# Another order for layer 3's side steps in a four-layer kernel: when they are issued beside the scan, which decay comes first, and the norm within one chunk

## The chip, the cores and the metric

The kernel runs on one core of a Trainium2 chip. The metric is the time of one launch on the device in microseconds (us): the median of several runs, and beside it the one execution that the hardware profiler recorded. Five engines work side by side, each in the order of its own instruction stream: PE (TensorE, matmuls), DVE (VectorE), ACT (ScalarE), POOL (GpSimd) and SP (SyncE), which here issues all DMAs.

## The reference, cut to what matters

Four layers run one after the other on an input of 4 images, 128 channels, 64 x 64 points: an attention with a threshold, a selective scan, a softmax attention, and a selective scan in both directions with a group norm. The change is about the last one and about the scan loop that layers 1 and 3 share.

```python
u = silu(conv(u) + conv_b)                       # 256 inner channels, from xf @ Win
x_dbl = u @ Wx                                   # dt (8), Bm (16), Cm (16)
delta = softplus(dt @ Wdt + bdt)
dA  = exp(delta * A)                             # for each channel and each of 16 states
dBu = delta * Bm * u
h = dA_l * h + dBu_l                             # step by step along 16384 points
y = sum over states of h * C_l
y = (y + u * D) * silu(z)
out = y @ Wout                                   # forward pass plus flipped backward pass
xn = (xg - mu) * rsqrt(var + 1e-5) * gn_w + gn_b # 4 groups of channels in each image
return silu(xn) + x
```

## The kernel before

Layer 3 (`layer3`, from line 1423) cuts the 16384 points into 16 chunks of T = 1024 and goes through them forward, then backward: 32 chunks, numbered 0 to 31 below. A chunk has J = 2 blocks (two halves of the 256 channels), and a block 16 tiles. A tile holds 128 rows, 8 channels times 16 states, by 1024 points. So a chunk has 32 tiles, numbered 0 to 31 below, and the layer 1024. Layer 1 has the same number of tiles, 256 for each image, in blocks that are summed four by four.

`scan_stream` (line 640) is the loop over tiles. All its engines are pinned to the program's order (`InOrder`, line 101), so what is written first is done first on each engine. For tile i it does, in this order:

- `carried(i - 2)`: ACT copies the last column of h to the carry, and with that lets go of the h buffer (four of them);
- `spread(i + 1)`: two matmuls put the rows of du of the next tile on all its partitions, in one of two PSUM buffers named db;
- `decayed_apart(i + 1)` and then `decayed(i + 2)`: ACT's exponentials. Every fourth tile (i % 4 == 3) is "apart": there the rows of delta are taken from PSUM and the decay is done in place (db<-db), the rows of du come by DMA, and POOL multiplies them by B (`driven`, x<-row, three tiles ahead). In all others the rows of delta come by DMA (da<-row), and DVE multiplies db by B;
- `load_for(i + 3)`: SP issues the next loads of rows, 512 KB each, into five buffers. That gives the row of tile i + 5 unless it is apart, and the row of tile i + 6 if it is apart;
- DVE's product (not if apart) and the scan; POOL's product of h and C (p<-h);
- the loads of B and C for the next block at n == 6 of a block (`reps`);
- at n == 4 `begun`: two matmuls start the sums of a block with u times D;
- the side steps of this tile; then, in every fourth tile, `summed`: 16 matmuls add four older tiles' p.

When a block is over, `done` multiplies silu(z) by its sums on DVE, at n == 3 of the next block.

The side steps of layer 3 are written out by tile in a plan (`into`, line 1708; `run`). Steps of one tile run in the order in which they were added: those of `prep` are added at the start, those of `post` and `finish` when a chunk ends. `prep(K)` (line 1469) gives the steps that make chunk K's inputs, during the chunk before it: `taps` and `silu(.., "u")` for u, `rows_a` and `rows_b` for B, C and dt, `step_a` and `step_b` for delta, then `time_steps` (line 788) for each block as todo(j, 0) to todo(j, 6), and `gate` with `silu(.., "z")`. The seven todo steps are:

- 0, `times`: SP stores 96 rows of delta, POOL computes du = delta * u, SP stores 32 rows of du;
- 1, `other`: ACT copies delta over those 32 rows of du. It can only run when the store has read them;
- 2, `high`: ACT casts to bf16;
- 3 and 5, `minus`: PE computes what the cast left over, in the two PSUM banks named misc; 4 and 6, `rest`: ACT casts that. After 6, SP issues 12 DMAs that place the three bf16 parts in `parts`, which `spread` reads.

`post(K)` (line 1566) makes the chunk's output (o_ps, yo) and stores it; `finish(b)` (line 1592) runs when a backward chunk completes an image: it loads the image's four tiles of r, sums them, takes the mean, loads them again for the squares, computes scale and shift, and loads them a third time for silu, the residual (POOL) and the store. yo, r and res share two SBUF buffers (`scratch`). Three images finish beside the scan of later chunks, and the last one after the scan. A plan entry above 31 falls in the chunk after.

Of the kernel before, what the change touches and what calls it, by code (L numbers as in the profile page):

```python
# [115 lines left out]
class Net:  # L116
# [523 lines left out]
    def scan_stream(self, pools, blocks, side, early=lambda k, n: None):  # L640

        pe, dve, act, pool, sp = self.pinned()  # L650
        rows, tmp, psd, pst = pools
        S, E = self.SPREAD, self.EIGHT
        O, Q, G = S // E, P // S, P // E

        order = [q * O + o for o in range(O) for q in range(Q)]
        items = [(k, n) for k in range(len(blocks)) for n in range(G)]
        W = self.T
        AHEAD = 3
        db, da, p, h, row = {}, {}, {}, {}, {}
        total = {}  # L660

        def apart(i):
            return i % Q == Q - 1

        def of(i):
            k, n = items[i]
            return blocks[k], order[n]

        def decay(t, src, i):
            B, g = of(i)  # L670
            act.activation(t, src, AF.Exp, scale=B.decay[:, g : g + 1])
            da[i] = t

        def spread(i):

            if i < len(items):
                B, g = of(i)
                db[i] = psd.tile([P, W], F32, name="db", tag="db")
                for j in range(W // NB):
                    s = bass.ts(j, NB)  # L680
                    pe.matmul(db[i][:, s], self.sel[:, g % O, :], B.parts[:, g // O, s], start=True, stop=True)

        def decayed(i):
            if i < len(items) and not apart(i):
                decay(tmp.tile([P, W], F32, name="da", tag="da"), row.pop(i), i)

        def decayed_apart(i):
            if i < len(items) and apart(i):
                t = db.pop(i)
                decay(t, t, i)  # L690

        def load(i):
            if i < len(items):
                B, g = of(i)
                row[i] = rows.tile([P, W], F32, name="row", tag="row", bufs=5)
                from_ = B.rows[g * E : (g + 1) * E, :]
                sp.dma_start(out=row[i], in_=from_.unsqueeze(0).to_broadcast([G, E, W]))

        def load_for(t):

            if not apart(t + 2):
                load(t + 2)
            if apart(t + AHEAD):
                load(t + AHEAD)

        x = {}

        def driven(i):
            if i < len(items) and apart(i):
                x[i] = tmp.tile([P, W], F32, name="x", tag="x", bufs=1)  # L710
                pool.tensor_tensor(x[i], row.pop(i), of(i)[0].b_rep, ALU.mult)

        def begun(B):
            if B.first:
                B.totals[0] = pst.tile([P, W], F32, name="total", tag="total")
                for j in range(W // NB):
                    s = bass.ts(j, NB)
                    pe.matmul(B.totals[0][:, s], B.diag_d, B.u[:, s], start=True, stop=False)

        def summed(i):  # L720

            k, n = items[i]
            B = blocks[k]
            for j in range(W // NB):
                s = bass.ts(j, NB)
                for m in range(i, i + Q):
                    g = of(m)[1]
                    r = (g // O) * S
                    pe.matmul(
                        B.totals[0][r : r + S, s], self.gather[:, g % O, :], p[m][:, s],  # L730
                        start=False, stop=(B.last and n == G - Q),
                    )
            for m in range(i, i + Q):
                del p[m]

        def carried(i):
            B, g = of(i)
            act.copy(B.carry[:, g : g + 1], h[i][:, B.at : B.at + 1])
            del h[i]

        blocks[0].reps()
        for i in range(-2, AHEAD):
            load_for(i)
        spread(0)
        decayed(0)
        decayed(1)
        for i, (k, n) in enumerate(items):
            B, g = of(i)
            if i > 1:
                carried(i - 2)  # L750
            spread(i + 1)
            decayed_apart(i + 1)
            decayed(i + 2)
            load_for(i + AHEAD)
            if not apart(i):
                x[i] = db.pop(i)
                dve.tensor_tensor(x[i], B.b_rep, x[i], ALU.mult)
            if n == 3 and k and blocks[k - 1].last:
                blocks[k - 1].done(blocks[k - 1].totals.pop(0))
            early(k, n)  # L760
            h[i] = tmp.tile([P, W], F32, name="h", tag="h", bufs=4)
            dve.tensor_tensor_scan(
                h[i][:, B.way], da[i][:, B.way], x[i][:, B.way], B.carry[:, g : g + 1], ALU.mult, ALU.add,
            )
            del da[i], x[i]
            p[i] = tmp.tile([P, W], F32, name="p", tag="p", bufs=7)
            pool.tensor_tensor(p[i], h[i], B.c_rep, ALU.mult)
            driven(i + AHEAD)
            if n == 6 and k + 1 < len(blocks):
                blocks[k + 1].reps()  # L770
            if n == 4:
                begun(B)
            side(k, n)
            if i % Q == 1 and i > Q:
                summed(i - 1 - Q)
        carried(len(items) - 2)
        carried(len(items) - 1)
        summed(len(items) - Q)
        blocks[-1].done(blocks[-1].totals.pop(0))

# [642 lines left out]
    def layer3(self):  # L1423
# [4 lines left out]
        with self.pool("l3w", 1) as big, self.pool("l3", 2) as work, self.pool("l3t", 2) as tmp, \  # L1428
# [40 lines left out]
            def prep(K):  # L1469
# [82 lines left out]
                def todo(j, i):  # L1552
# [3 lines left out]
                    8: [begin, taps(0, 0)], 10: [taps(0, 1)], 11: [silu(0, "u")],  # L1556
                    12: [taps(1, 0)], 14: [taps(1, 1)], 15: [silu(1, "u")],
                    16: [rows_a], 17: [rows_b], 18: [step_a(0)], 19: [step_b(0)],
                    20: [todo(0, 0)], 21: [todo(0, 1)], 22: [todo(0, 2), step_a(1)], 23: [step_b(1)],
                    24: [todo(1, 0), todo(0, 3)], 25: [todo(0, 4)],  # L1560
                    26: [todo(1, 1), gate(0)], 27: [silu(0, "z")],
                    28: [todo(1, 2), todo(0, 5)], 29: [todo(0, 6)],
                    30: [gate(1)], 31: [silu(1, "z")],
                }, {0: [todo(1, 3)], 1: [todo(1, 4)], 2: [todo(1, 5)], 3: [todo(1, 6)]}

            def post(K):
                lo = K.ch * T
                held = {}

                def a(c):  # L1570
                    def go():
                        held[c] = misc("o_ps")
                        for j in range(J):
                            pe.matmul(held[c], self.WoutT[:, j, :], K.sz[:, j, bass.ts(c, NB)], start=(j == 0), stop=(j == J - 1))
                    return go

                def b():
                    t = scratch("yo")
                    for c in range(C):
                        s = bass.ts(c, NB)  # L1580
                        if K.forward:
                            act.copy(t[:, s], held[c])
                        else:
                            dve.tensor_tensor(t[:, s], held[c], K.yf[:, s], ALU.add)
                    sp.dma_start(out=self.y3[:, lo : lo + T], in_=t)

                slots = {4: [a(0)], 6: [a(1)], 7: [b]}
                if not K.forward and lo % L == 0:
                    slots |= finish(lo // L)
                return slots  # L1590

            def finish(b):
# [66 lines left out]
                        sp.dma_start(out=self.out[b, :, bass.ts(m, T)], in_=r)  # L1659
                    return go  # L1660

                slots = {20: [over_group("sum"), mean], 52: [over_group("dev")], 53: [scale], 54: [shift]}
                for at, f in ((8, sums), (22, squares)):
                    for m in range(M + 1):
                        slots[at + m] = ([f(m - 1)] if m else []) + ([part(m)] if m < M else [])
                for m in range(M):
                    slots[55 + 3 * m] = [part(m)]
                    slots[56 + 3 * m] = [silus(m)]
                    slots[57 + 3 * m] = [outs(m)]
                return slots  # L1670

            chunks = []
            for forward in (True, False):
                for ch in range(NT) if forward else reversed(range(NT)):
                    K = Chunk()
                    K.ch, K.forward, K.number, K.turn = ch, forward, len(chunks), len(chunks) % 2
                    K.blocks = []
                    for j in range(J):
                        B = Block()
# [36 lines left out]
            for i, K in enumerate(chunks):  # L1716
                now, gates = prep(K)
                into(i - 1, now)
                into(i, gates)
                if i > 1:  # L1720
                    into(i - 2, {4: [lambda K=K: fetch(K)]})
                else:
                    fetch(K)
                if not K.forward:
                    into(i, {NS: [lambda K=K: behind(K)]})
# [102 lines left out]
```

## Time and profile before

| what | us |
|---|---|
| median of 3 runs | 11183.19 (11176.51 to 11188.2) |
| the profiled execution | 11183.87 |
| its span, first to last instruction | 11182.1 |
| layer 3: first scan starts | 7254.8 |
| layer 3: last scan ends | 11103.1 |
| chunk 3 (forward), first scan to next chunk's first scan | 7603.55 to 7719.85 |
| layer 1's scans, four images | 863.3, 903.1, 903.4, 892.5 |

| engine | busy us | share of the span |
|---|---|---|
| PE | 8629.2 | 77% |
| DVE | 9239.8 | 83% |
| ACT | 6252.6 | 56% |
| POOL | 8143.9 | 73% |

The time is the device's time for one launch; the span is what lies between the first and the last instruction that the profiler recorded, so 1.8 us lie around it. A group's line in the page gives the line of the source (L111 is the helper through which every pinned instruction passes, so groups are told apart by the names of their tiles), the engine, the operation, what it writes and reads with shapes, the count, then busy time and mean duration of one in ns, and last the idle time of the engine just before these instructions with what ended most of it. An arrow points to what was waited for: "<-ACT db" is a wait until ACT had written db. A timeline line gives the start, the duration, the engine, and in brackets the idle time before it. SP's lines show when a DMA was issued, not when it landed.

### The profile page before, as it was taken

To read this page: it belongs to the slowest core of one execution; us is meant where nothing else is said; L and a number is where in the kernel's file an instruction comes from. 1 tells how busy PE (TensorE), PEld (TensorE's weight loads), DVE (VectorE), ACT (ScalarE), POOL (GpSimd) and SP (SyncE) were. 2 spreads that over 40 slices of the span, in tenths; PEclk is the share of its full clock that TensorE was granted. 3 is DMA by queue.
4 is the path that set the end of the run, shared out by engine and by line. 5 is a ranking of instruction groups with operands and counts; after the bars stand their busy time and mean duration, and the time that the engine had idled before them with its cause. 6 is when DMAs were issued, how large, how long until landed. Compare 5 with 4: busy or idle time off the path is not lost. (4 is left out here: it accounts for less than half of the span.)

```text
span 11182.1 us, 91225 instructions
## 1 busy us (share of the span) xinstructions
PE 8629.2 (77%) x28104; PEld 3091.9 (28%) x28104; DVE 9239.8 (83%) x6438; ACT 6252.6 (56%) x9435; POOL 8143.9 (73%) x3566
## 2 busy tenths in 40 slices
PE   8986668987787997787997877877777777766665
PEld 3331113332222332222332222322222222222221
DVE  7859997869997876997886997198888988888876
ACT  3324445646664655664664665456566565656564
POOL 6748885748886766886774886088888888777776
PEclk9997779998998998998998988888888888878887
DMA  1017771008872006874005885177777777778776
GB/s 28 15 48 190 191 175 32 15 26 204 202 195 61 17 12 169 204 197 105 15 13 122 201 200 134 41 190 184 191 180 188 189 186 192 195 188 199 191 197 164
DMA packets 502953, 1522.34 MB, mean 136 GB/s; under 512 B 83432, under 2 KB 91144, under 8 KB 502464
## 3 DMA queue, kind: packets, MB, share of 16 engines
q1 hardware_dynamic: 502464, 1516.51, 54.9%
q8 instruction: 223, 3.65, 0.1%
q14 instruction: 266, 2.18, 0.1%
HBM read 1327.38 MB, written 125.94 MB: 130 GB/s over the span
## 5 line engine op out<-in xcount | busy, mean ns | idle before, releaser
L111 POOL TENSOR_TENSOR p<-h,c_rep 128x1024 f32<-128x1024 f32 x2048 | 4808.0, 2356 | 1312.4 <-DVE h L111 1209.8
L111 DVE TENSOR_TENSOR_SCAN h<-da,carry,db 128x1024 f32<-128x1024 f32 x1536 | 3603.4, 2346 | 232.7 <-ACT da L111 50.9
L111 PE MATMUL db<-parts,sel 96*128 96x512 bf16 x4096 | 1414.4, 432 | 1587.9 <-DVE h L111 1443.2
L111 DVE TENSOR_TENSOR db<-b_rep,db 128x1024 f32<-128x1024 f32 x1536 | 1856.5, 1209 | 399.3 <-PE db L111 217.8
L111 ACT ACTIVATE da<-row,A 128x1024 f32<-128x1024 f32 x1536 | 1752.8, 1144 | 127.0 <-DMA row<-d 126.8
L111 POOL TENSOR_TENSOR e<-e,bound 128x1024 f32<-128x1024 f32 x512 | 1242.1, 2428 | 567.2 <-DVE e L111 567.1
L111 ACT ACTIVATE db<-db,A 128x1024 f32<-128x1024 f32 x512 | 556.9, 1088 | 1779.6 <-PE db L111 1736.0
L111 DVE TENSOR_TENSOR_SCAN h<-db,carry,x 128x1024 f32<-128x1024 f32 x512 | 1194.7, 2333 | 201.6 <-ACT db L111 195.9
L111 POOL TENSOR_TENSOR x<-row,b_rep 128x1024 f32<-128x1024 f32 x512 | 1207.5, 2358 | 6.3 <-DMA row<-d 6.3
L111 PEld LDWEIGHTS <-sel 96*128 96x128 bf16 x4096 | 325.4, 102 | 3083.1 <-DVE h L111 1694.9
L111 PE MATMUL total<-p,gather 128*32 128x512 f32 x8192 | 1158.7, 679 | 21.0 <-POOL p L111 21.0
L111 PE MATMUL lg<-q,k 128*128 128x512 f32 x2048 | 1026.2, 625 | 153.6 <-DVE e L111 153.2
L111 ACT ACTIVATE e<-e 128x1024 f32<-128x1024 f32 x512 | 540.9, 1057 | 1046.9 <-POOL e L111 1046.9
L111 PE MATMUL acc<-e,values 128*128 128x512 f32 x1536 | 884.1, 668 | 180.7 <-ACT e L111 157.6
L111 PE MATMUL acc<-t,vT 128*128 128x512 f32 x2048 | 955.9, 593 | 6.4 <-DVE t L111 3.3
L111 DVE TENSOR_TENSOR t<-lg,ncut 128x1024 f32<-128x1024 f32 x512 | 624.8, 1220 | 292.3 <-PE acc L111 260.5
L111 ACT ACT_TABLE_LOAD x593 | 760.8, 1283 | 99.0 <-DMA r<-y 71.6
L111 POOL TENSOR_TENSOR t<-t,e 128x1024 f32<-128x1024 f32 x256 | 609.8, 2382 | 47.4 <-ACT t L111 47.4
L111 ACT ACTIVATE e<-gq,below,fcol 128x512 f32<-128x512 f32 x768 | 609.9, 805 | 60.6 <-PE acc L111 60.3
L111 PE MATMUL rest_ps<-du,ident 128*128 128x512 f32 x640 | 480.0, 842 | 206.0 <-ACT sz L111 120.4
L111 ACT ACTIVATE junk<-gp,ntop,fcol 128x512 f32<-128x512 f32 x768 | 619.5, 807 | 27.6 <-DMA gp<-g 14.9
L111 DVE SCALAR_TENSOR_TENSOR e<-t,lg 128x1024 f32<-128x1024 f32 x512 | 619.1, 1209 | 2.5
(214 smaller groups left out, 10085.3 us busy)
## 6 DMA issues: line engine op xcount, KB each, us to landing
row<-d SPq DMA_DIRECT2D x2048, 512.0 KB
parts<-split SPq DMA_DIRECT2D x960, 64.0 KB
b_rep<-bc SPq DMA_DIRECT2D x96, 512.0 KB
c_rep<-bc SPq DMA_DIRECT2D x96, 512.0 KB
d<-delta SPq DMA_DIRECT2D x80, 384.0 KB
r<-y SPq DMA_DIRECT2D x48, 512.0 KB
xq<-in_x SPq DMA_DIRECT2D x64, 256.0 KB
q<-q SPq DMA_DIRECT2D x64, 256.0 KB
```

Of the source, the lines that this page charges most:

```text
L111: return self.tc.keep_in_program_order(method(*args, **kwargs))
```

## The change

Four things change.

In `scan_stream` the two matmuls of `begun` move from tile n == 4 of a block, ahead of the side steps, to just before the block's first `summed`, which comes after the side steps of tile n == 5. And `decayed(i + 2)` is issued before `decayed_apart(i + 1)`, no longer after it. Both touch layers 1 and 3.

In `prep` the steps from tile 20 on are laid out anew. `other` of block 0 moves from tile 21 to tile 23, three tiles behind `times`; `times` of block 1 moves from 24 to 22; all `rest` steps of both blocks end at tiles 27 and 31, where before block 1's last four steps ran in tiles 0 to 3 of the chunk itself. The gates change places with them: they move from tiles 26 to 31 of the chunk before into tiles 0, 2, 6 and 7 of the own chunk.

In `post` and around it the output matmuls and yo move from tiles 4, 6, 7 to 3, 4, 5, and the load of xt for the chunk after next from tile 4 to 7.

In `finish` the norm of an image, which ran over tiles 8 to 66 counted from the chunk after the image's last, runs over tiles 6 to 37: sums in 6 to 10, mean in 17, squares in 18 to 22, the group's deviation in 24, scale and shift together in 25, the last pass in 26 to 37. No operation is added or dropped.

```diff
-        def begun(B):
-            if B.first:
+        def summed(i):
+
+            k, n = items[i]
+            B = blocks[k]
+            if n == 0 and B.first:
                 B.totals[0] = pst.tile([P, W], F32, name="total", tag="total")
                 for j in range(W // NB):
                     s = bass.ts(j, NB)
                     pe.matmul(B.totals[0][:, s], B.diag_d, B.u[:, s], start=True, stop=False)
...
             spread(i + 1)
+            decayed(i + 2)
             decayed_apart(i + 1)
-            decayed(i + 2)
             load_for(i + AHEAD)
...
-            if n == 4:
-                begun(B)
             side(k, n)
...
-                    20: [todo(0, 0)], 21: [todo(0, 1)], 22: [todo(0, 2), step_a(1)], 23: [step_b(1)],
-                    24: [todo(1, 0), todo(0, 3)], 25: [todo(0, 4)],
-                    26: [todo(1, 1), gate(0)], 27: [silu(0, "z")],
-                    28: [todo(1, 2), todo(0, 5)], 29: [todo(0, 6)],
-                    30: [gate(1)], 31: [silu(1, "z")],
-                }, {0: [todo(1, 3)], 1: [todo(1, 4)], 2: [todo(1, 5)], 3: [todo(1, 6)]}
+                    20: [todo(0, 0), step_a(1)], 21: [step_b(1)], 22: [todo(1, 0)], 23: [todo(0, 1), todo(0, 2)],
+                    24: [todo(0, 3)], 25: [todo(0, 4)], 26: [todo(0, 5), todo(1, 1)],
+                    27: [todo(0, 6), todo(1, 2)], 28: [todo(1, 3)], 29: [todo(1, 4)], 30: [todo(1, 5)],
+                    31: [todo(1, 6)],
+                }, {0: [gate(0)], 2: [silu(0, "z")], 6: [gate(1)], 7: [silu(1, "z")]}
...
-                slots = {4: [a(0)], 6: [a(1)], 7: [b]}
+                slots = {3: [a(0)], 4: [a(1)], 5: [b]}
...
-                slots = {20: [over_group("sum"), mean], 52: [over_group("dev")], 53: [scale], 54: [shift]}
-                for at, f in ((8, sums), (22, squares)):
+                slots = {17: [over_group("sum"), mean], 24: [over_group("dev")], 25: [scale, shift]}
+                for at, f in ((6, sums), (18, squares)):
                     for m in range(M + 1):
                         slots[at + m] = ([f(m - 1)] if m else []) + ([part(m)] if m < M else [])
                 for m in range(M):
-                    slots[55 + 3 * m] = [part(m)]
-                    slots[56 + 3 * m] = [silus(m)]
-                    slots[57 + 3 * m] = [outs(m)]
+                    slots[26 + 3 * m] = [part(m)]
+                    slots[27 + 3 * m] = [silus(m)]
+                    slots[28 + 3 * m] = [outs(m)]
...
-                    into(i - 2, {4: [lambda K=K: fetch(K)]})
+                    into(i - 2, {7: [lambda K=K: fetch(K)]})
```

More of the change, by code (lines that the diff above doesn't have):

```diff
@@ L718, in begun @@
                     pe.matmul(B.totals[0][:, s], B.diag_d, B.u[:, s], start=True, stop=False)
-        def summed(i):
-            k, n = items[i]
-            B = blocks[k]
             for j in range(W // NB):
```

## The prediction

> **What bounds the kernel now.** I read the page first, then the vector engine's waits over layer 3, then one chunk's timeline, then the DMA share in stretches of it. The page's groups:
>
> ```profile
> L111 POOL TENSOR_TENSOR p<-h,c_rep 128x1024 f32<-128x1024 f32 x2048 | 4808.0, 2356 | 1312.4 <-DVE h L111 1209.8
> L111 DVE TENSOR_TENSOR_SCAN h<-da,carry,db 128x1024 f32<-128x1024 f32 x1536 | 3603.4, 2346 | 232.7 <-ACT da L111 50.9
> L111 DVE TENSOR_TENSOR db<-b_rep,db 128x1024 f32<-128x1024 f32 x1536 | 1856.5, 1209 | 399.3 <-PE db L111 217.8
> L111 ACT ACTIVATE da<-row,A 128x1024 f32<-128x1024 f32 x1536 | 1752.8, 1144 | 127.0 <-DMA row<-d 126.8
> L111 ACT ACTIVATE db<-db,A 128x1024 f32<-128x1024 f32 x512 | 556.9, 1088 | 1779.6 <-PE db L111 1736.0
> ```
>
> The reader is to see that three tiles of four need a product and a scan on DVE (1.21 + 2.35, 3.60 from scan start to scan start), while the "apart" tile needs a scan alone (2.26 to the next). Four tiles take 13.0 us on DVE, and on POOL 4 x 2.36 + 2.36 = 11.8. DVE is the bound wherever nothing makes it wait. A chunk of 32 tiles without waits is chunk 31, the last, which prepares nothing: scan starts 10996.72 to the end of its last scan at 11103.13, 106.4, which with the missing 1.2 of a next product and without its own 1.2 for yo is also a forward chunk's floor. Chunks 1 to 19 take 115.7 to 117.9, mean near 116.4. So some 9.9 us in each are waits. The waits of DVE, then of ACT, in layer 3 (total us, times, longest):
>
> ```profile
> DVE db L111 <- PE db L111: 200.5, 114, 8.3
> DVE h L111 <- ACT db L111: 154.7, 44, 8.5
> ...
> ACT du L111 <- DMA d<-du: 334.1, 45, 10.8
> ```
>
> Where they lie is read from chunk 3's scan starts: tile 22 to 23 takes 6.65 (floor 2.26), 25 to 26 4.67 (3.60), 29 to 30 4.52 (3.60), 31 to the next chunk's 0 7.03 (3.57): 4.4 + 1.1 + 0.9 + 3.5 = 9.9, all of it. The timeline at the first:
>
> ```profile
> 7678.07 2.34 POOL L111 TENSOR_TENSOR du<-delta,u 128x1024 f32<-128x1024 f32 x1
> 7678.13 2.35 DVE L111 TENSOR_TENSOR_SCAN h<-da,carry,db 128x1024 f32<-128x1024 f32 x1
> ...
> 7680.44 0.31 SPq L111 DMA_DIRECT2D d<-du  x1
> ...
> 7680.80 1.17 SPq L111 DMA_DIRECT2D row<-d  x2
> 7682.06 0.54 SPq L111 DMA_DIRECT2D b_rep<-bc  x1
> 7682.44 1.04 ACT L111 COPY du<-delta 32x1024 f32<-32x1024 f32 x1 [10.53 <-DMA d<-du]
> ...
> 7684.78 2.35 DVE L111 TENSOR_TENSOR_SCAN h<-db,carry,x 128x1024 f32<-128x1024 f32 x1 [4.31 <-ACT db L111]
> ```
>
> ACT reaches the copy over du's rows (tile 21) early, waits 10.53 us for the store of those rows, and tile 23's decay stands behind it: scan 23 is 4.3 late. In that time SP stands at the same store, and the DMA engines idle and are then full (stretches before and after it):
>
> ```profile
> 7671.00:7680.40 9.40, 8.16 (x28) 2.11 (x26) 9.13 (x5) 0.91 (x2) 8.11 (x5) 0.82 0.04 17
> 7680.40:7697.00 16.60, 8.65 (x28) 2.51 (x28) 10.96 (x8) 11.68 (x17) 13.09 (x7) 0.59 0.93 221
> ```
>
> The last two columns are DMA share and GB/s.
>
> **What the Trainium skill says.** "DMA: Bandwidth & Descriptors", Queues, rings and completion order: all that SP issues runs on one row of rings, and each DMA engine takes its descriptors in ring order, so a load waits for the bytes queued ahead. The trace agrees: in chunk 20 row and xt loads start issuing at 9602.91 and 9603.60, the next row's at 9604.17, and ACT's decay on the latter waits until 9611.56, 7.4 us for 1.5 MB ahead and own, where a lone 128 KB store lands in under 2.0 (7680.44 to the copy at 7682.44). The same page, Anatomy of one DMA: the semaphore wait is on the issuing sequencer; the 0.04 share above agrees. "TensorE: Matmul & The Clock Gate", Part 1: after an idle window of about 3.4 us the array runs slower; here a db pair takes 1.01 after 6.05 us idle (7687.19) and 0.60 otherwise (7676.93).
>
> **The change, part by part.** I write times from scan 22 of chunk 3 (7678.13 = 0). The floor has scan 23 due at 2.26, 24 at 5.84, 25 at 9.44, 26 at 13.04, 27 at 15.30.
>
> (1) The copy goes from tile 21 to 23, its cast from 22 to 23. Store issue is 2.31 and landing 4.3. ACT gets to tile 23 after decay 23. For that decay, PE carries de_ps(1) in tile 20 and in tile 21 the diag pair (1.9 warm; it took 2.9 at tile 4 after idling) and the gather sums (1.92), so spread(23) ends near 1.0 and the decay near 2.1, due 2.26. Minus 4.4, with 0 to 0.5 left over. ACT then waits under 1 us for the store with nothing behind it that is due (decay 26 is due at 13).
>
> (2) minus(0) follows the cast directly (about 6.5 to 10), no longer a softplus at tile 23; product 26 is due at 11.8: minus 1.1. At tile 29 the gate's PE work and its silu, 2 x 1.28 table loads + 2 x 0.6, no longer hold the two misc banks: minus 0.9. parts(0) goes out at tile 27, not 29, and is landed two tiles before spread(32): minus 3.5.
>
> (3) times(1) goes from tile 24 to 22, past SP's loads of rows 28 and 29 and in front of POOL's p(23). POOL then runs without a gap: du(0) to 2.28, p21 4.6, p22 6.9, du(1) 9.25, p23 11.6, p24 13.95, x(27) 16.3. x(27) is due at 15.3: plus 1.0. SP waits for du(1) until 9.3, and only then issues row 28. Ahead of it in the ring: w store 128 KB, rows 26 and 27, b_rep, c_rep at 512 KB, delta(1) 384 KB, w(1) 128 KB; with itself 3200 KB = 3.28 MB. At 221 GB/s from 2.3 that is 14.8 us: row 28 lands near 17.3.
>
> (4) The decay order. In tile 26 ACT now does da(28), which needs row 28, before the in-place decay of 27. So 17.4 + 1.14 + 1.09 + 0.1 gives scan 27 at 19.7, not 15.3: plus 4.4, which covers the 1.0 of x(27). With the old order it would have been the 1.0 alone. Behind the waiting da stand decay 27, the copy of du(1), rest(2) and parts(0) (then near 29, needed at tile 31). Elsewhere the da fits the idle time before the in-place decay (1779.6 / 512 = 3.5 us each), and its row was issued some 15 us before: nothing. Bounds of this step: 1.0 (row in time) to 6 (row 28 at 200 GB/s).
>
> A forward chunk: 116.4 - 9.9 + 4.4 + 0.1 = 111.0, so 5.4 less in each of the 31 chunks that prepare a next one: 167.
>
> (5) The gates in tiles 0, 2, 6, 7 of the own chunk: ACT is idle there by 3 to 5 us at a time (before the copies of the carry); 3.8 us of silu after the decay of tile 3 or 7 delays nothing due within a tile. Post two or three tiles earlier and xt three later: same instructions, nothing. The diag pair at tile 5 with the gather sums: spread(7) ends near 1.5 after scan 5, the decay 1.1 later, due at 3.5: nothing; likewise at the first blocks of layer 1. Layer 1's in-place decays wait for PE, not ACT: 0, bounds -5 and +5.
>
> (6) The norm. Three images are normalised inside the stream. The first one's chunks, 20 to 22, took 131, 132.7 and 129.2 where ordinary backward chunks take 117.4: 40.7 an image. After, its loads of r share SP and the ring with (3). Worked the same way: sums in tiles 7 to 10 stand before tile 11's decay, +6, and push silu(u) and taps(1,0) as now, +4.5 (now 5.4 in all); nmean 1.3 (now 1.3); r for squares(2) is issued behind the w store, lands near 6.5, and decay 23 waits: +8; scale and shift in one slot behind a full ACT +5 (one wait of 4.6 now), less 4.4 since row 28 is then in time; the silu chain, 10.2 us a tile of r in the tail (store, load, silu, add) against three tiles, about 17, and yo at tile 37, which takes the buffer of the r just sent out, 3. Sum near 41: no change, bounds -15 and +15 each, 45 in all.
>
> (7) Before the first scan parts(1) now precedes b_rep on SP: 12 issues of 0.63 less the gates' 7.6 us of ACT: plus 3. The tail after 11103 keeps its order: nothing.
>
> Sum: 11183.9 (the profiled execution; its span is 11182.1, the median of the runs 11183.2, so no correction) - 167 + 3 + 0 = 11020.
>
> **The rivals.**
> Row 28 in time: the ring is faster than 221, or SP is less far behind. Then only x(27)'s 1.0 stays: 8.8 per chunk, 273, and 11183.9 - 273 + 3 = 10914. For it: the old order never shows da(28) waiting. Against: 16.6 us at 0.93 share without a gap.
>
> The norm eats more: each of its loads waits on a fuller ring and yo's buffer holds DVE; +25 an image or more, 75: 11095. For it: ACT's 12.4 and 6.4 us waits for r in chunk 21.
>
> Slower: the ring becomes the bound. A chunk moves 21.7 MB (187 GB/s over 116 us); SP's store wait leaves 9.4 us of it idle. A chunk then needs 21.7 / rate + 9.4, and this decides against the change below 203 GB/s (21.7 / 107.0). At 195 it is 120.7 a chunk, +4.3 x 31 = 133: 11317. For it: the stretch with parts (7697 to 7715) moved 204 at 0.89. Against: 21.7 / 0.221 + 9.4 = 107.6, under 111.
>
> That the plan does nothing, other waits of 9.9 coming up, is the last: 11184.
>
> **How the numbers follow.** Row 28 late 0.55 (10975 to 11065: 1.5 us a chunk either way); in time 0.22 (10870 to 10955); the norm 0.12 (11065 to 11130); the ring 0.08; nothing 0.03. 0.2% of the time, 22 us, is about what a measurement of this kernel tells from no change. Faster 0.89, same 0.03, slower 0.08. The range is from 10885 to 11120.
>
> **What would show it.** Scan 22 to 23 at 2.3 to 2.8; scan 26 to 27 at 6 to 7, with ACT's da idle for a DMA of row before it; ACT's wait for d<-du under 2 us a chunk; tiles 25, 29, 31 at the floor; chunks near 111; the norm's three chunks near 377 in sum. Wrong: tile 26 at 2.3 to 3.3 (row in time), or 22 still above 5 (spread(23) late on PE), or a DMA share near 0.93 through whole chunks.

## The result, and the profile after

The median went from 11185.69 us (11176.51 to 11188.86) to 11016.55 us (11003.12 to 11020.47), each from four runs on one chip: a ratio of 0.9848, 95% interval 0.9831 to 0.9865. The profiled execution after took 11020.47 us; its span is 11018.7 us, 163.4 us less than before. The groups of the page after, in the order in which those of before were shown (busy us, mean ns of one, then the idle time just before them and what ended most of it):

```profile
L111 POOL TENSOR_TENSOR p<-h,c_rep 128x1024 f32<-128x1024 f32 x2048 | 4807.0, 2356 | 1169.4 <-DVE h L111 1101.9
L111 DVE TENSOR_TENSOR_SCAN h<-da,carry,db 128x1024 f32<-128x1024 f32 x1536 | 3603.9, 2346 | 191.5 <-ACT da L111 47.5
...
L111 ACT ACTIVATE da<-row,A 128x1024 f32<-128x1024 f32 x1536 | 1761.9, 1147 | 711.9 <-DMA row<-d 710.0
L111 DVE TENSOR_TENSOR db<-b_rep,db 128x1024 f32<-128x1024 f32 x1536 | 1855.1, 1208 | 222.8 <-DMA b_rep<-bc 187.1
...
L111 ACT ACTIVATE db<-db,A 128x1024 f32<-128x1024 f32 x512 | 555.4, 1085 | 1223.4 <-PE db L111 1210.6
```

No mean duration here has moved by more than 3 ns, only idle time. DVE waits 177 us less before its products (399.3 to 222.8). ACT's decay on loaded rows waits 585 us more for a DMA (127.0 to 711.9), and the one in place 556 us less for PE. That fits the swapped order: in every fourth tile ACT now reaches the row's decay first, and stands there for the row where it stood at the in-place decay for PE. The waits in layer 3, of DVE, of ACT and of SP's queue (total us, times, longest):

```profile
DVE h L111 <- ACT db L111: 152.1, 38, 9.6
DVE h L111 <- ACT carry L111: 59.9, 32, 2.8
...
DVE db L111 <- PE db L111: 28.3, 26, 4.7
...
ACT da L111 <- DMA row<-d: 523.8, 197, 13.9
...
SPq L111 <- POOL du L111: 458.1, 62, 12.1
```

ACT's 334.1 us at the copy over du's rows are 1.4, and DVE's 200.5 us for PE are 28.3. But DVE still waits 152.1 us for the in-place decay, as before. Where that is, the scan starts say. Means over chunks 1 to 15, as excess over the floor, which is what a tile takes from its scan start to the next when nothing waits (2.26, or 3.5 to 3.6):

| | chunk | tile 22 | tile 25 | tile 26 | tile 29 | tile 31 |
|---|---|---|---|---|---|---|
| before | 116.37 | +4.41 | +0.80 | 0 | +1.27 | +3.16 |
| after | 110.86 | +2.25 | 0 | +2.50 | 0 | 0 |

Tiles 25, 29 and 31 have lost their waits; of tile 22's wait one half is still there, and the other half has come up at tile 26. Chunk 3, around both (PE, ACT, SP, DVE in turn; the two matmuls of de_ps or of u times D count as x4):

```profile
7624.47 3.78 PE L111 MATMUL de_ps<-bc,Wdt 8*128 8x512 f32 x4
7628.18 1.03 PE L111 MATMUL db<-parts,sel 96*128 96x512 bf16 x2
7629.00 3.37 PE L111 MATMUL total<-u,diagD 128*128 128x512 f32 x4
7632.31 1.92 PE L111 MATMUL total<-p,gather 128*32 128x512 f32 x16
7634.16 1.04 PE L111 MATMUL db<-parts,sel 96*128 96x512 bf16 x4
...
7634.81 1.09 ACT L111 ACTIVATE db<-db,A 128x1024 f32<-128x1024 f32 x1 [3.28 <-PE db L111]
...
7649.38 1.15 ACT L111 ACTIVATE da<-row,A 128x1024 f32<-128x1024 f32 x1 [5.84 <-DMA row<-d]
7650.44 1.07 ACT L111 ACTIVATE db<-db,A 128x1024 f32<-128x1024 f32 x1
...
7622.05 0.32 SPq L111 DMA_DIRECT2D d<-delta  x1
7634.17 0.31 SPq L111 DMA_DIRECT2D d<-du  x1
...
7641.09 0.31 SPq L111 DMA_DIRECT2D d<-du  x1
7641.45 7.10 SPq L111 DMA_DIRECT2D row<-d  x5
...
7636.00 2.35 DVE L111 TENSOR_TENSOR_SCAN h<-db,carry,x 128x1024 f32<-128x1024 f32 x1 [1.81 <-ACT carry L111]
7638.26 1.21 DVE L111 TENSOR_TENSOR db<-b_rep,db 128x1024 f32<-128x1024 f32 x1
7639.51 2.35 DVE L111 TENSOR_TENSOR_SCAN h<-da,carry,db 128x1024 f32<-128x1024 f32 x1
...
7651.61 2.35 DVE L111 TENSOR_TENSOR_SCAN h<-db,carry,x 128x1024 f32<-128x1024 f32 x1 [2.55 <-ACT db L111]
```

The same two pairs in chunk 3 of the kernel before:

```profile
7670.55 3.62 PE L111 MATMUL total<-u,diagD 128*128 128x512 f32 x4
...
7677.46 1.98 PE L111 MATMUL de_ps<-bc,Wdt 8*128 8x512 f32 x4
```

Tile 22: PE runs from 7624.47 to spread(23), the db<-parts at 7634.16, without a gap. The pair of u times D was slow before too (3.62, in tile 20, where it made nothing late); now de_ps is slow as well (3.78 for 1.98), and the other pair (3.37) comes right behind it. So spread(23) is late, the decay starts at 7634.81, and scan 23 at 7636.00, not at 7634.10. Tile 26: ACT stands 5.84 us at da(28) for row 28, with the in-place decay of 27 behind it; scan 27 starts 19.77 after scan 22 (7631.84).

The 163.4 us by place (first scan to last scan): layer 3 is 131.5 shorter (3848.4 to 3716.9), layer 1 is 31.3 (3562.2 to 3530.9), what lies between layer 1 and layer 3 is 1.8, the tail 0.7, and some 2 net are given back elsewhere. Within layer 3, forward chunks 0 to 15 give 87.5, the six ordinary backward chunks 29.2, and the nine chunks with a norm in them only 15.6. The norm's surplus, an image's three chunks against three ordinary ones, was 40.9, 40.4 and 40.2 an image and is 51.8, 51.6 and 46.4.

### The profile page after: what moved, and what is told of

The parts are those of the page before. It is cut to its first block, busy times and chain, and to the rows that moved or that the text cites. A ratio compares the mean times of both kernels' runs of the same rounds, so it can differ in the third digit from the quotient of the medians.

```text
span 11018.7 us, 90651 instructions
## 1 busy us (share of the span) xinstructions
PE 8625.8 (78%) x28025; PEld 3091.5 (28%) x28104; DVE 9229.1 (84%) x6438; ACT 6294.7 (57%) x9435; POOL 8142.2 (74%) x3566
## 5 line engine op out<-in xcount | busy, mean ns | idle before, releaser
L111 ACT ACTIVATE da<-row,A 128x1024 f32<-128x1024 f32 x1536 | 1761.9, 1147 | 711.9 <-DMA row<-d 710.0
L111 DVE TENSOR_TENSOR db<-b_rep,db 128x1024 f32<-128x1024 f32 x1536 | 1855.1, 1208 | 222.8 <-DMA b_rep<-bc 187.1
L111 PE MATMUL total<-p,gather 128*32 128x512 f32 x8192 | 1182.7, 691 | 17.4 <-POOL p L111 17.4
L111 DVE TENSOR_TENSOR t<-t,fl 128x1024 f32<-128x1024 f32 x512 | 614.8, 1210 | 2.1 <-PE fl L111 2.1
```

What stands on the lines that cost most here:

```text
L111: return self.tc.keep_in_program_order(method(*args, **kwargs))
```

## The experiments

Each kernel is the changed one but for the edit shown, and each ran in three rounds against the kernel before on the same chip, whose median was 11173 to 11182 us (11185.69 on the chip of the changed kernel). So a difference of two medians from different chips is good to some 10 us, and the ratios tell more. "Chunk" is the mean of chunks 1 to 15 in the profiled execution, with the largest of its tiles over the floor.

| run | median us | ratio, 95% | chunk | over the floor |
|---|---|---|---|---|
| (after) | 11016.55 | 0.9848 [0.9831, 0.9865] | 110.86 | 22: 2.25, 26: 2.50 |
| e1_apart_first_l3 | 11011.38 | 0.9847 [0.9832, 0.9861] | 110.81 | 22: 2.03, 1: 0.80, 29: 0.44, 6: 0.38 |
| e3_reps_tile26 | 11055.23 | 0.9883 [0.9866, 0.9899] | 111.77 | 1: 2.41, 22: 2.02, 30: 0.56, 6: 0.38 |
| e4_begun_tile3 | 11031.61 | 0.9865 [0.9850, 0.9880] | 111.27 | 26: 4.09, 22: 0.53, 4: 0.46 |
| e5_begun3_reps26 | 11047.26 | 0.9881 [0.9866, 0.9895] | 111.91 | 1: 2.26, 26: 1.28, 30: 1.18, 9: 0.41 |
| a1_copy_tile21 | 11031.50 | 0.9871 [0.9856, 0.9886] | 111.44 | 22: 5.45 |
| c1_parts_tile29 | 11077.61 | 0.9914 [0.9897, 0.9930] | 112.56 | 26: 2.33, 22: 2.27, 31: 1.94 |
| e7_store_later | 10933.18 | 0.9781 [0.9764, 0.9797] | 108.24 | 22: 2.30 |
| e9_store_later_begun3 | 10926.05 | 0.9772 [0.9757, 0.9786] | 108.08 | 26: 0.80, 4: 0.44, 22: 0.29 |
| b1_store_later_times24 | 10875.11 | 0.9732 [0.9718, 0.9747] | 106.73 | 4: 0.34, 29: 0.21 |
| b2_and_old_norm | 10892.84 | 0.9751 [0.9735, 0.9767] | 106.52 | 4: 0.28 |
| e6_norm_old_slots | 11009.24 | 0.9847 [0.9832, 0.9862] | 110.72 | 26: 2.42, 22: 2.22 |
| e2_apart_first_l1 | 11055.29 | 0.9887 [0.9873, 0.9902] | 110.85 | 26: 2.79, 22: 2.06 |

### First four: take one suspected wait away

The decay order back in layer 3 alone (a flag that only layer 3 sets):

```diff
+            if three:
+                decayed_apart(i + 1)
             decayed(i + 2)
-            decayed_apart(i + 1)
+            if not three:
+                decayed_apart(i + 1)
```

> The changed kernel with the old order of the two decays in layer 3 alone (layer 1 keeps the new one). Theory: tile 27's in-place decay is held by da(28), which stands before it and waits for its row; with the old order scan 26 to 27 returns from 4.7 us (median of the forward chunks) to 2.3 to 2.7 and ACT's waits of da for row move behind it at no cost: about -2.3 x 28 = -65 in the chunks, and +16 because the scan of tile n % 4 == 0 waits for ACT again (0.06 x 256). Sum -50: near 10967. Rival, that PE or POOL's x(27) holds scan 27: tile 26 stays at 4.7 and only the +16 comes: near 11033.

The loads of B and C four tiles later, and the matmuls of u times D at tile 3 of a block, both in layer 3 alone:

```diff
-            if n == 6 and k + 1 < len(blocks):
+            if n == (10 if three else 6) and k + 1 < len(blocks):
```

> The changed kernel with layer 3's loads of B and C for the next chunk at tile 26 rather than 22; nothing else. Theory: row 28 is late because 1 MB of B and C stand before it in the ring; without them it lands 4.5 us earlier, and scan 26 to 27 falls from 4.7 to 2.3 to 3.0 (x(27) on POOL may leave some tenths): -2 x 28 = -55, near 10960. Rival, that SP's wait for the store of du's rows alone makes row 28 late, or that something else holds scan 27: tile 26 stays above 4, time within 10 of 11017.

```diff
-            if n == 0 and B.first:
+            if n == 0 and B.first and not three:
...
+            if three and n == 3:
+                begun(B)
             side(k, n)
```

> The changed kernel with the two matmuls of u times D at tile n == 3 of a block in layer 3, right after the DVE product that frees the sums' bank, rather than at n == 5. Theory of tile 22: PE, slowed after idling, still has these two matmuls (3.4 us) before the sums and spread(23), so scan 22 to 23 takes 4.5; in tile 19 PE idles, so 22 falls to 2.3 to 2.8. Theory of tile 26: the time of row 28 is set by scan 22, POOL and the ring, not by scan 23, so tile 26 rises by what 22 loses, to 6.3 to 7: time within 15 of 11017. Rival, that the stall at 26 is a fixed extra: 26 stays at 4.7 and the time falls by 2 x 28 = 55 to 10960.

And both of these together:

> Both edits at once: matmuls of u times D at n == 3, loads of B and C at tile 26, in layer 3. Theory: now both waits go, 22 at 2.3 to 2.8 and 26 at 2.3 to 3.5 (x(27) is due 2 us earlier, POOL then ends up to 1 us late): -3.6 x 28 = -100, near 10915. Rival, that the two stalls are one and the same delay on POOL that moves on: 26 or a later tile keeps 2 or more and the time stays above 10950.

Each took its own wait away (the last one leaves 1.28 at tile 26) and none took time away; the two with B and C at tile 26 are slower than the change, and their intervals lie above its own. With the old order, tile 26 is at its floor and the chunk is the same, 110.81: the wait is spread over tiles 1, 29, 6 and 4, and a wait of some 0.07 us is back in each of eight tiles (see the last section). With the matmuls at tile 3, tile 22 falls by 1.7 and tile 26 grows by 1.6. With B and C at tile 26, tile 26 falls by 2.4 and tile 1 grows by 2.4. Where time was to go by the theory (10967, 10960 and 10915 in the first, second and fourth run), none went; the third was to stay within 15 us of 11017 and is 14.6 above it.

The wait that walks, at tiles 26, 1, 29 and 30, is in the main ACT's decay waiting for a row (86 us in the fifteen chunks before tile 1, with B and C at tile 26), and one queue brings all rows. So its cause was to be looked for upstream of those tiles. Tile 22 is another matter: there PE is late. In the run with the matmuls at tile 3, block 1's de_ps takes 3.78 us in six of the fifteen chunks and 1.98 to 2.26 in nine; in the six, tile 22 takes 3.37 to 3.72, in the nine 2.26. There the pair of u times D stands in the slow stretch in de_ps's place, as it did before the change.

### Undo one part of the change

The copy over du's rows back at tile 21, and the cast at 22:

```diff
-20: [todo(0, 0), step_a(1)], 21: [step_b(1)], 22: [todo(1, 0)], 23: [todo(0, 1), todo(0, 2)],
+20: [todo(0, 0), step_a(1)], 21: [step_b(1), todo(0, 1)], 22: [todo(1, 0), todo(0, 2)],
```

> The changed kernel with one part undone: du(0)'s copy over its rows back at tile 21 and its cast at 22, in front of the store's landing, as in the kernel before. By the prediction's step 1 the wait at tile 22 is 4.4 again where it is 2.2 in the changed kernel, and scan 23 starts 2.2 later: 31 x 2.2 = 68 slower, 11085. The theory that has grown since (scan 27 waits for row 28, and row 28 for the release of SP by du(1) and for the bytes before it, which POOL gives whether scan 23 is late or not): scan 23 is later, scan 27 is not, tile 26 falls by what tile 22 gains, a chunk stays near 110.8, and the total within 15 of 11017.

The timeline of chunk 3 in this run, ACT then DVE:

```profile
7655.29 1.04 ACT L111 COPY du<-delta 32x1024 f32<-32x1024 f32 x1 [5.89 <-DMA d<-du]
...
7658.68 2.35 DVE L111 TENSOR_TENSOR_SCAN h<-db,carry,x 128x1024 f32<-128x1024 f32 x1 [5.36 <-ACT db L111]
...
7671.66 2.32 DVE L111 TENSOR_TENSOR_SCAN h<-db,carry,x 128x1024 f32<-128x1024 f32 x1
```

ACT stands at the store again, and scan 23 is 5.4 late. But scan 27 is then on time: tile 26 is at the floor in all fifteen chunks, and the chunk is 0.58 longer, not 2.2. The ratio's interval overlaps that of the change. So in this kernel the move of the copy is worth some 0.58 x 31 = 18 us (the medians differ by 15 us; by the ratios it is 26), because the late row 28 comes right behind it.

The transfers of block 0's parts two tiles later (twelve of them, not six as the expectation says):

```diff
...
-27: [todo(0, 6), todo(1, 2)], 28: [todo(1, 3)], 29: [todo(1, 4)], 30: [todo(1, 5)],
-31: [todo(1, 6)],
+27: [todo(0, 6), todo(1, 2)], 28: [todo(1, 3)], 29: [todo(1, 4), todo(0, 7)], 30: [todo(1, 5)],
+31: [todo(1, 6), todo(1, 7)],
```

> The changed kernel with one part undone: the six transfers of parts(0) are issued at tile 29 and not right behind the split at tile 27 (parts(1) likewise behind the split at 31, unmoved); the split itself stays. By the prediction's step 2, parts(0) is then late for the first gather of the next chunk again: tile 31 takes 7.0 instead of 3.5, 31 x 3.5 = 108 slower, 11125. Rival (the late row absorbs this wait as it absorbed the others, or the parts still land in time): within 20 of 11017. Between the two, some 1 to 2 us a chunk, if the two tiles of slack that the changed kernel has are only just used up.

Here todo(j, 7) issues the twelve transfers, and time does come back: 61 us (74 by the ratios), tile 31 is 1.94 over its floor, and 31 x 1.94 = 60. Of before's 3.16 at this tile that is six tenths; the split itself, which was later before too, stays early in this run. The outcome lies between the two that were expected, 108 us or none. This is the largest single part of the gain that a run gives back.

### What stands upstream: SP at the store of du

```diff
         def times():
...
             pool.tensor_tensor(w, delta, u, ALU.mult)
-            sp.dma_start(out=B.rows[Z:, :], in_=w[Z:, :])
+            if not later:
+                stored()
+
+        def stored():
+            sp.dma_start(out=B.rows[Z:, :], in_=held["w"][Z:, :])
...
-        return steps
+        return steps + [stored]
...
-22: [todo(1, 0)],
-24: [todo(0, 3)],
+22: [todo(1, 0), todo(0, 7)],
+24: [todo(0, 3), todo(1, 7)],
```

> The store of du's rows leaves the step that multiplies du and is issued two tiles later (tile 22 for du(0), tile 24 for du(1)), so that SP no longer stands at it with the loads of rows behind it. Theory (the ring has a hole while SP stands at the store, some 10 us a chunk at tiles 18 to 22 at a DMA share of 0.02, and is full for the rest of the chunk; whatever was moved so far only moved the late load): the hole is filled, row 28 is in time, scan 26 to 27 falls from 4.7 to the floor 2.26, and 31 chunks of 2.4 us go: 11017 - 75 = 10942, with the wait at tile 22 (PE late) staying. Rival (the rate of the ring alone bounds a chunk at 110.5, hole or not): chunks stay at 110 to 111, another tile takes the wait, 11000 to 11020.

> As the run with the store two tiles later, and in layer 3 the matmuls of u times D go back to tile 3 (they stand at tile 5 in the changed kernel), so that PE has none of them between spread(22) and spread(23). Theory: with the hole gone both waits go, tile 22 and tile 26 at 2.3 each, chunks near 106.8: 11017 - 31 x 4.1 = 10890. Rival (the rate of the ring alone bounds a chunk): 11000 to 11020. In between, 10942 or so, if the matmuls only move PE's lateness elsewhere.

In these two kernels layer 1 runs the added step too: it stores its 32 rows of du a second time, when they hold delta, and so scans with other numbers and does not compute what the reference does. Layer 3's instructions are as described, and layer 1's scans take 3538 and 3535 us, as in the other kernels. The windows of chunk 3 from just before scan 20 on, in the changed kernel (last three columns: TensorE clock granted, DMA share, GB/s):

```profile
7624.00:7634.20 10.20, 10.20 (x29) 3.09 (x28) 9.89 (x6) 5.83 (x8) 8.95 (x5) 0.61 0.07 27
7634.20:7652.00 17.80, 11.67 (x45) 4.38 (x43) 13.15 (x8) 9.50 (x14) 17.80 (x8) 0.90 0.98 238
```

and with the store two tiles later:

```profile
7626.00:7636.20 10.20, 10.20 (x30) 3.28 (x30) 9.63 (x6) 5.67 (x9) 8.96 (x5) 0.66 0.99 253
7636.20:7654.00 17.80, 12.83 (x44) 4.73 (x43) 16.37 (x10) 14.08 (x21) 17.80 (x8) 0.89 0.60 145
```

What SP issues there, and its wait for du in layer 3 (458.1 us, at most 12.1 at a time, in the changed kernel):

```profile
7624.16 2.70 SPq L111 DMA_DIRECT2D row<-d  x2
7626.95 0.54 SPq L111 DMA_DIRECT2D b_rep<-bc  x1
7627.55 0.59 SPq L111 DMA_DIRECT2D c_rep<-bc  x1
7630.74 0.31 SPq L111 DMA_DIRECT2D d<-delta  x1
7635.90 0.31 SPq L111 DMA_DIRECT2D d<-du  x1
...
SPq L111 <- POOL du L111: 293.3, 59, 5.3
```

In the changed kernel ten us pass in which the DMA engines do next to nothing (0.07), and then eighteen in which they are full (0.98). SP has come to the store of du(0) after its last issue at 7622.05, but POOL makes du(0) only from 7631.78 to 7634.14, and the rows of two tiles and B and C stand behind the store until 7634.17. With the store later, those loads fill the ten us (0.99), and the next eighteen need 0.60. Tile 26 is at the floor in every chunk, the chunk is 2.6 shorter, the total 83 (75 by the ratios): the theory's 75 and not the rival's 0. The Trainium skill has it in "DMA: Bandwidth & Descriptors", Queues, rings and completion order, that SP's DMAs run on one row of rings, from which each DMA engine takes its descriptors in ring order; nothing but the order of issue was changed in layer 3, and it was worth 2.6 us a chunk.

The edit moves both stores of a chunk, and row 28 is now issued 3.3 us after scan 22 instead of 9.6. No run moves one store alone. An estimate from the prediction's bytes and 221 GB/s: with the second store alone moved, row 28 would be spared only the 128 KB of that store ahead of it, 0.6 us. So it is the hole that is likely to count, by this estimate and not by a run.

With the matmuls at tile 3 as well, tile 22 is nearly clear, but a 0.80 is left at tile 26 and 0.44 at tile 4, and 7 us are gained where 52 more were expected. DVE's waits in layer 3 of that run:

```profile
DVE h L111 <- POOL x L111: 16.2, 19, 0.9
```

x(27) comes 0.9 late, behind du(1) in POOL's order, which the prediction had as its "plus 1.0". So du(1) goes to tile 24, behind x(27), its store to 26, its copy to 27:

```diff
-22: [todo(1, 0), todo(0, 7)],
-24: [todo(0, 3), todo(1, 7)],
-26: [todo(0, 5), todo(1, 1)], 27: [todo(0, 6), todo(1, 2)],
+22: [todo(0, 7)],
+24: [todo(0, 3), todo(1, 0)],
+26: [todo(0, 5), todo(1, 7)], 27: [todo(0, 6), todo(1, 1), todo(1, 2)],
```

In this kernel layer 1 stores its rows once, as in the changed kernel, and computes the same numbers as it.

> The run with the later store and the matmuls of u times D at tile 3, and in it du(1) multiplied at tile 24 (after POOL's x(27)) instead of 22, stored at 26 and copied at 27. Theory (what is left at tile 26 there, 3.26 for 2.26, is POOL's x(27) behind du(1), the 1.0 us of the prediction's step 3): tile 26 at 2.3, 31 x 0.8 = 25 less, 10926 - 25 = 10900. Rival (the wait goes to another tile, as it did with a late row): within 8 of 10926.

The same line in this run, with the one that led the list after the change:

```profile
DVE h L111 <- ACT db L111: 52.3, 10, 9.9
...
DVE h L111 <- POOL x L111: 1.0, 2, 0.5
```

Tiles 22 and 26 are at 2.26 in all fifteen chunks. Seven chunks take 105.9, which is the floor of 106.4 less eight waits of 0.06 that the new order drops; four take 108.5 to 108.8, with waits at tiles 4, 9 and 29 whose cause wasn't sought, and the mean is 106.73. The total is 10875.11, 0.9732 [0.9718, 0.9747] of the kernel before, 51 below the run without this step (45 by the ratios) where 25 were expected: of the 1.35 a chunk, tile 26 gave 0.80, tile 22 0.29, and small waits at tiles 1 to 11 the rest. This is the fastest version of the study.

### The norm and layer 1

The norm in its old slots (the five lines of the diff in `finish` taken back), alone and in the fastest version:

> The changed kernel with the norm of a finished image in its old slots (sums from tile 8, squares from 22, scale and shift at 53 and 54, the last pass from 55). Theory (the norm in one chunk costs some 10 us an image more than before): 3 images x 10 = 30 less, 10987; the three finishing chunks of an image take 378 in sum and not 389. Rival (it is the fuller ring that costs the norm more, wherever its slots are): within 10 of 11017.

> As the run with du(1) at tile 24, and the norm of an image in its old slots. If the norm's extra wait in one chunk is its crowded slots: 3 x 5 = 15 less than that run. Rival (the old slots gain only by giving way to the late row, which is gone here): within 8 of it. Should the finishing chunks be the longer for it, the new slots are the better ones once the ring's hole is gone.

The norm's surplus is 46.0, 47.3 and 48.6 an image with the old slots, against 51.8, 51.6 and 46.4; the ratio of the run is that of the change. In the fastest version it is 46.3, 51.5 and 48.3 against 43.0, 52.1 and 44.2, with overlapping intervals of the total. Neither gives the 30 and 15 us that a crowded chunk would have cost, so the choice of slots makes no difference that these runs can tell. Why the norm costs some 6 to 9 us an image more than before in all four, on average, wasn't settled. One possibility that no run tests: before, part of what the norm costs lay inside waits that each chunk had anyway (9.9 us, 4.75 after).

The old decay order in layer 1 alone (the edit of the first run, with the flag the other way round):

> The changed kernel with the old order of the two decays in layer 1 alone (decay in place first), layer 3 as changed. Layer 1's scans took 3562 us in four images before and 3531 to 3547 in the runs with the new order. Theory (the order drops one wait of 0.063 us in front of every fourth tile's scan, 256 of them in layer 1, and nothing else): layer 1 goes up by 16 and the total to 11033. Rival 1 (the whole gain of layer 1 is the order): layer 1 back at 3562, the total 11040 to 11048. Rival 2 (layer 1's gain is the place of the matmuls of u times D): layer 1 stays near 3535, 11017.

Layer 1's scans take 3573.8 us, where the change has 3530.9 and the eleven other kernels with the new order 3532 to 3547. That is beyond all three outcomes that were expected: all of the 31 us go with the order, and the place of u times D gives nothing here. The 12 us above the kernel before may be chance, as the twelve kernels with the new order lie up to 16 apart. The last section has what about half of the gain is.

## Why the prediction was right, and where it was wrong

The total was right: 11020 predicted for an execution that took 11020.47 (the median is 11016.55). The forward chunk was right by its mechanism: 111.0 predicted, 110.86 measured. The rest was wrong in three sizes, two of which cancel by luck.

- **Step 2, tiles 25, 29 and 31**: as predicted, all three at the floor, and the run with late transfers gives 60 us of it back. This is where the change's gain in a chunk is, 5.2 of 5.5 us; tiles 22 and 26 together hold what tile 22 held.
- **Steps 3 and 4, row 28**: the mechanism and the size from scan 22 were right. SP's second store was issued 9.25 after scan 22 (9.3 predicted), da(28) began at 17.54 (row to land near 17.3) and scan 27 started at 19.77 (19.7). The surplus at tile 26 is 2.5 and not 4.4, because scan 23, from which it counts, was late already; the sum over both tiles is 4.75, near the predicted 4.4 + 0 to 0.5.
- **Step 1, the term that was mis-sized**: "with 0 to 0.5 left over" at tile 22 is 2.25. The prediction priced the diag pair at 1.9 warm and gave de_ps, ahead of it, no price; they took 3.37 and 3.78, one behind the other in one run of PE. Not only its "2.9 at tile 4 after idling" was a warning: in the kernel before the pair of the second block took 3.45 on average and 3.62 in the very chunk that was worked through, and was what stood in PE's slow stretch ahead of de_ps. The run with the matmuls at tile 3 puts it back there: tile 22 falls to 0.53 over, and what is left is in the chunks where de_ps is slow. What this wait costs on its own was nothing, as long as row 28 was late: the same run is not faster.
- **Step 5, layer 1 at 0**: it gave 31.3. The order of the decays was priced by whose data come last; half of the gain is a semaphore less for a scan to wait on (last section), the other half isn't explained.
- **Step 6, the norm at 0**: 11 us more for each of two images and 6 for the third, 28 in all, inside the stated bounds of 45. Only some 3 an image fall away with the old slots, so the term was wrong for a reason other than the slots that it counted.
- **Step 7**: minus 1.8 for plus 3; nothing follows from it.

In sum: layer 3 was to give 167 and gave 131.5, layer 1 was to give 0 and gave 31.3. Nearly all that layer 3 lacks is in the nine chunks with a norm (15.6 given, 9 x 5.4 = 49 forecast). That the total fits to a microsecond is chance: the two errors have nothing to do with each other.

Of the rivals, "row 28 in time" was not this kernel, but its working was sound: with only x(27)'s 1.0 left a chunk was to take 107.6, and the kernel with the row in time and 0.80 left at tile 26 takes 108.08. "The norm eats more" was to cost 25 us an image or more, and it cost 6 to 11. "The ring becomes the bound" fell: the fastest version moves the same 21.7 MB in 106.73 us, 203 GB/s, and has both tiles at the floor. But its mechanism, a hole in the ring and the catching up after it, is what made row 28 late; only the rate was not the limit.

## What to carry to other kernels

When a wait is removed and comes up a few tiles on at the same size, stop moving the waiting instructions and look for a resource that all those places share: put the DMA share beside the scan starts and look for a stretch near 0 followed by one near 1. A queue whose issuing engine reaches a store before its data exist is such a place; issue the store where the data are ready, and the loads that need not wait ahead of it. And price a moved step with everything it stands between on each engine: the move of the copy was worth some 18 us of 163, and the transfers moved along with it some 60.

## What the runs showed of the hardware that was not expected

Swapping two ACT instructions shortens DVE's stream. With the in-place decay first, the scan of a tile behind an apart one waits on ACT and on DVE. With the row's decay first, the scan before it has already waited for a later instruction of ACT (the in-place decay), so its own wait on ACT is not needed; that it is left out for this reason is argued, but the count fits: DVE's semaphore instructions fall from 3225 to 2726, one for almost each of the 512 tiles behind an apart one. The timeline of DVE in chunk 3 before, an apart scan and what follows:

```profile
7698.89 2.32 DVE L111 TENSOR_TENSOR_SCAN h<-db,carry,x 128x1024 f32<-128x1024 f32 x1
7701.13 1.21 DVE L111 TENSOR_TENSOR db<-b_rep,db 128x1024 f32<-128x1024 f32 x1
7702.44 2.35 DVE L111 TENSOR_TENSOR_SCAN h<-da,carry,db 128x1024 f32<-128x1024 f32 x1
```

From the product's end (7702.34) to the scan are 0.10 us; in the changed kernel, in the lines 7638.26 and 7639.51 shown above, 0.04. The mean over such tiles, without gaps of 0.3 us and more, is 91.6 ns before and 28.2 after; 0.063 x 512 = 32 us, half in each of layers 1 and 3. The two runs that take the old order back in one layer bring the gap back in that layer alone: a median of 104 ns there and of 36 in the other, with 2981 semaphore instructions (layer 3) and 2966 (layer 1). Of layer 1's 31 us this is 16. Of the rest, DVE's products wait 17.0 us for PE in the four images' scans before and 6.6 after, while its scans' waits for the in-place decay are no shorter (40.8 and 48.7); why wasn't settled.

PE stays slow through a stretch in which it doesn't idle. The changed kernel in chunk 3 (windows as above, and the end of the gap in PE's timeline):

```profile
7620.00:7622.00 2.00, 0.60 (x2) 0.21 (x3) 2.00 (x3) 1.99 (x3) 1.83 (x2) 0.94 1.03 262
7622.00:7624.00 2.00, 0.47 (x2) 0.10 (x1) 2.00 (x2) 1.97 (x4) 1.04 (x2) 0.50 1.03 240
...
7630.00:7632.00 2.00, 2.00 (x4) 0.53 (x2) 1.87 (x3) 1.51 (x3) 2.00 (x2) 0.50 0.00 0
7632.00:7634.00 2.00, 2.00 (x17) 0.42 (x16) 2.00 (x1) 0.00 (x0) 2.00 (x1) 1.00 0.00 0
...
7623.53 1.01 PE L111 MATMUL db<-parts,sel 96*128 96x512 bf16 x2 [2.76 <-DVE h L111]
```

PE idles 1.09 us, does 0.60 us of work at 7620.16, and idles 2.76 us until 7623.53. The granted clock falls to 0.50 just before 7622, within that gap, and is 1.00 again only from 7632 on, though PE has worked without a gap since 7623.53. In between the four matmuls of de_ps take 3.78 us where they took 1.98 in the kernel before. The Trainium skill, "TensorE: Matmul & The Clock Gate", Part 1, has such a slow stretch follow an idle window of about 3.4 us; here no single gap was that long, and the slow stretch lasted 10 us.
